# Group norm statistics spread over four slots, with the input loaded earlier, in a pre-activation lookup-convolution block

## The chip, the cores and the metric

The kernel runs on one core of one Trainium2 chip. The core has five engines that each work through their own queue of instructions in order: TensorE (PE), which multiplies matrices into PSUM; VectorE (DVE); ScalarE (ACT); GpSimd (POOL); and SyncE (SP), which here only starts transfers. POOL starts transfers too. The engines wait for one another through semaphores. The metric is the time of one execution on the device in microseconds (us).

## What is computed

For 16 images of 256 channels and 28 x 28 pixels the block takes a group norm of x, passes it through two 3x3 "lookup" convolutions, scales by a squeeze-and-excitation gate and adds x twice:

```python
def amm_conv3x3(x, centroids, w_sub, stride=1):      # C=256, k=16, s=9
    patches = jax.lax.conv_general_dilated_patches(x, (3, 3), (stride, stride), 'SAME')
    p = patches.reshape(B, C, s, Ho * Wo).transpose(0, 3, 1, 2)
    d = (jnp.sum(p * p, axis=-1)[..., None] - 2.0 * jnp.einsum('bncs,cks->bnck', p, centroids)
         + jnp.sum(centroids * centroids, axis=-1)[None, None])
    attn = jax.nn.softmax(-d, axis=-1)
    lut = jnp.einsum('cks,cso->cko', centroids, w_sub)
    out = jnp.einsum('bnck,cko->bno', attn, lut)
    # ...
def _gn(v, G=32, eps=1e-5):
    g = v.reshape(B_, G, C_ // G, H_, W_)
    m = jnp.mean(g, axis=(2, 3, 4), keepdims=True)
    s = jnp.var(g, axis=(2, 3, 4), keepdims=True)
    return ((g - m) / jnp.sqrt(s + eps)).reshape(v.shape)
# block(v):  out = relu(bn1(amm_conv3x3(v)));  out = bn2(amm_conv3x3(out));  out = se(out);  relu(out + v)
# result:    x + block(_gn(x))
```

A group is 8 channels of 784 pixels. With 128 channels on the partitions, its statistics need a reduction along each partition (DVE) and one across 8 partitions (PE, a product with a block-diagonal matrix).

## The kernel before

The kernel is written as a plan of jobs. Each job has a slot and a position within the slot; when the plan is laid out, the jobs are emitted in the order of slot and position, and each lands at the end of its own engine's queue. A stage (one convolution of one image) has 16 slots, one per unit of 32 channels and half the pixels. Stages of layer 0 and layer 1 alternate, so an image takes 32 slots.

```python
LOGITS, LOAD, MOVE, EXP, LOOK_A, NUM, TURN, SMALL, LOOK_B, MAX, LOOK_C, TURN_BACK, REST = range(13)
NS = len(PXT) * NQ                                    # 16
...
# for a unit at slot s:
at(s, LOGITS, b_logits, u)          # PE, L578: 16 matmuls into two PSUM pairs
at(s, EXP, b_exp, u)                # ACT, L636
at(s + 1, NUM, b_num, u)            # PE, L646: 16 matmuls into two PSUM pairs
at(s + 1, TURN, b_turn, u)          # DVE: two transposes out of PSUM (L658), reciprocal (L664)
at(s + 1, TURN, c_scale, u)         # POOL: L674, L680, running sums L686
at(s + 2, TURN_BACK, c_turn, u)     # DVE: L692, for every fourth unit also qt L699
# the products with the tables (PE, L710) of other units lie at LOOK_A, LOOK_B, LOOK_C
```

There are three PSUM pairs in a ring. Logits of one slot and numerators of the next take two each, so a pair must be emptied by ACT or DVE before PE can write it again. The tile of patches (pt) of a unit is loaded by SP three slots ahead; "maxed" units (two per half in layer 1) also go out to DRAM and back (dm) for their maxima.

Group norm of an image runs while the stages of earlier images fill PE. Its parts:

```python
xpool = ctx.enter_context(tc.tile_pool(name="xpool", bufs=2))

def load_x(b, xb):
    t = xpool.tile([P, NB, HW], F32, tag="xt", name="xt")
    nc.gpsimd.dma_start(t, xb.rearrange("(b p) n -> p b n", p=P))      # L148, 784 KB
    xs[b] = t

def gn_stats(b, k):                                                   # DVE
    if k == 0:
        gst[b] = small.tile([P, NB, 2], F32, name="gn_mv")
    st = small.tile([P, 2, 6], F32, name="gn_st")
    for i in range(2):
        nc.vector.bn_stats(st[:, i, :], xs[b][:, k, i * (HW // 2) : (i + 1) * (HW // 2)])   # L428
    nc.vector.bn_aggr(gst[b][:, k, :], st)                            # L429

def gn_mean(b):
    mv = gst[b]
    ps = spare()[:, : 2 * NB]
    nc.tensor.matmul(ps, lhsT=gmat, rhs=mv.rearrange("p b t -> p (b t)"), start=True, stop=True)  # PE, L434
    gm = small.tile([P, NB, 2], F32, name="gn_gm", bufs=6)
    nc.scalar.copy(gm.rearrange("p b t -> p (b t)"), ps)              # ACT, L436
    dv = small.tile([P, NB], F32, name="gn_dv")
    nc.gpsimd.tensor_sub(dv, mv[:, :, 0], gm[:, :, 0])                # POOL, L438
    nc.gpsimd.tensor_mul(dv, dv, dv)                                  # POOL, L439
    gst[b] = gm, dv

def gn_var(b):
    gm, dv = gst.pop(b)
    ps = spare()[:, :NB]
    nc.tensor.matmul(ps, lhsT=gmat, rhs=dv, start=True, stop=True)    # PE, L445
    # ... copy by ACT (L447); add, rsqrt, scale and shift by POOL (L448 to L453)

def gn_apply(b, k):                                                   # ACT, L458
    # ... ims[0] = x * rstd + nb

# in the plan, for image b, t = the anchor:
def norm(self, b, t):
    self.at(t, REST, gn_stats, b, 0)
    self.at(t + 1, REST, gn_stats, b, 1)
    self.at(t + 2, SMALL, gn_mean, b)
    self.at(t + 3, SMALL, gn_var, b)
    self.at(t + 4, REST, gn_apply, b, 0)
    self.at(t + 5, REST, gn_apply, b, 1)

# in the loop over stages, t = 16 * (stage number):
n0 = 3 if b == 1 else t - 2 * NS - 3
plan.at(n0 - (4 if b == 1 else 2), REST, load_x, b, x[b])
plan.norm(b, n0)
```

Image 0 is normalized ahead of the plan, image 1 in its first slots. x of an image is loaded a second time, for the residual, when its layer 1 is done.

Of the kernel before, what the change touches and what calls it, by code (L numbers as in the profile page):

```python
# [8 lines left out]
F32 = mybir.dt.float32  # L9
# [6 lines left out]
P = 128  # L16
H = W = 28
HW = H * W
# [52 lines left out]
def kernel(  # L71
# [32 lines left out]
    nc = tc.nc  # L104
    B, C, _ = x.shape
    NB = C // P
# [5 lines left out]
    small = ctx.enter_context(tc.tile_pool(name="small", bufs=3))  # L112
# [18 lines left out]
    def spare():  # L131

        return ring[(turn[0] + 1) % 3][:, 1]
# [10 lines left out]
    xs = {}  # L144

    def load_x(b, xb):
        t = xpool.tile([P, NB, HW], F32, tag="xt", name="xt")
        nc.gpsimd.dma_start(t, xb.rearrange("(b p) n -> p b n", p=P))  # L148
        xs[b] = t
# [270 lines left out]
    gst = {}  # L420
    nrm = {}

    def gn_stats(b, k):
        if k == 0:
            gst[b] = small.tile([P, NB, 2], F32, name="gn_mv")
        st = small.tile([P, 2, 6], F32, name="gn_st")
        for i in range(2):
            nc.vector.bn_stats(st[:, i, :], xs[b][:, k, i * (HW // 2) : (i + 1) * (HW // 2)])  # L428
        nc.vector.bn_aggr(gst[b][:, k, :], st)  # L429

    def gn_mean(b):
        mv = gst[b]
        ps = spare()[:, : 2 * NB]
        nc.tensor.matmul(ps, lhsT=gmat, rhs=mv.rearrange("p b t -> p (b t)"), start=True, stop=True)  # L434
        gm = small.tile([P, NB, 2], F32, name="gn_gm", bufs=6)
        nc.scalar.copy(gm.rearrange("p b t -> p (b t)"), ps)  # L436
        dv = small.tile([P, NB], F32, name="gn_dv")
        nc.gpsimd.tensor_sub(dv, mv[:, :, 0], gm[:, :, 0])  # L438
        nc.gpsimd.tensor_mul(dv, dv, dv)  # L439
        gst[b] = gm, dv  # L440
# [300 lines left out]
    LOGITS, LOAD, MOVE, EXP, LOOK_A, NUM, TURN, SMALL, LOOK_B, MAX, LOOK_C, TURN_BACK, REST = range(13)  # L741

    class Plan:
# [82 lines left out]
                self.at(t + 6 if dx == 1 else t + 7 + 3 * h + (i - n * h - NB) * 3 // 4, REST, to_pat, l, i, pat, *PXT[1])  # L826

        def norm(self, b, t):
            self.at(t, REST, gn_stats, b, 0)
            self.at(t + 1, REST, gn_stats, b, 1)  # L830
            self.at(t + 2, SMALL, gn_mean, b)
            self.at(t + 3, SMALL, gn_var, b)
            self.at(t + 4, REST, gn_apply, b, 0)
            self.at(t + 5, REST, gn_apply, b, 1)

        def close(self, b, ob, te, pace):
            self.at(te, SMALL, se_hidden, b)
# [12 lines left out]
    NS = len(PXT) * NQ  # L850
# [6 lines left out]
    def pat_of(l, b):  # L857
        return d_pat[2 * l + b % 2]
# [2 lines left out]
    row = sort_keys()  # L861
    square_codes(0)
    for k in range(NB):
        gn_stats(0, k)
    gn_mean(0)
    gn_var(0)
    sort_ranks(row)
# [9 lines left out]
    plan = Plan(1, 3, 6)  # L877
    for si, (l, b) in enumerate(stages):
        t = si * NS
        plan.stage(l, b, pat_of(l, b), t, () if l == 0 else MAXED)  # L880
        if l == 0 and b >= 1:
            n0 = 3 if b == 1 else t - 2 * NS - 3
            plan.at(n0 - (4 if b == 1 else 2), REST, load_x, b, x[b])
            plan.norm(b, n0)
            plan.prep(0, pat_of(0, b), {1: 9, 2: 33, 3: 57}.get(b, t - 2 * NS + 3), 0.67 if b == 1 else 1)
        if l == 1:
            if b in (0, B - 1):
                plan.prep_near(1, pat_of(1, b), t - NS + LC)
            else:
                plan.prep(1, pat_of(1, b), 45 if b == 1 else t - 2 * NS + LC + 1)  # L890
            plan.at(t + NS, REST, load_x, b, x[b])
            plan.close(b, out[b], t + NS + LC, 1 if b < B - 2 else 4)
# [25 lines left out]
    for i, lim in enumerate((S_MAX, 1.0 / S_MIN)):  # L918
        t = small.tile([P, 1], F32, name="ext")
# [9 lines left out]
    with tc.If(flag > 0):  # L929
        with tc.For_i(0, B) as bi:  # L930
            load_x("g", x[bass.ds(bi, 1)].rearrange("o c n -> (o c) n"))
            plan = Plan(8, 3, 6)
            plan.norm("g", 0)
            plan.prep(0, d_pat[0], 8)
            s0 = 32
            plan.stage(0, "g", d_pat[0], s0, range(NQ))
            plan.prep(1, d_pat[2], s0 + plan.end)
            s1 = s0 + plan.end + 24
            plan.stage(1, "g", d_pat[2], s1, range(NQ))
            plan.at(s1 + plan.end - 4, REST, load_x, "g", x[bass.ds(bi, 1)].rearrange("o c n -> (o c) n"))  # L940
            plan.close("g", out[bass.ds(bi, 1)].rearrange("o c n -> (o c) n"), s1 + plan.end, 1)
            plan.emit()
# [74 lines left out]
```

## Time and profile before

| | |
|---|---|
| time, median of three | 2895.39 us (2892.28 to 2902.37) |
| profiled span | 2894.4 us |
| PE busy | 2797.8 us, 97% |
| DVE busy | 2258.5 us, 78% |
| POOL busy | 1766.8 us, 61% |
| ACT busy | 1090.3 us, 38% |
| statistics passes (L428) | 64, mean 545 ns |
| aggregations (L429) | 32, mean 209 ns |
| load of x, issue to landing | 8.9 us in the median, 10.8 at most |

The profile names an instruction by its line, engine, operation and tiles, out<-in. Busy time is the union of an engine's instructions; idle time before an instruction is put down to whatever released it. A row of the waits reads "engine tile line <- what ended the wait: total us, times, longest us". A busy PE is not one at its peak, since matmuls overlap and their ends are modelled. The clock row gives the share of TensorE's full clock that was granted.

### The profile page before, as it was taken

What the parts mean: (1) busy time and instruction counts of PE and PEld (TensorE: products, weight loads), DVE (VectorE), ACT (ScalarE), POOL (GpSimd) and SP (SyncE); (2) the same over time, 40 slices, a digit from 0 to 9 for tenths busy, and PEclk for the clock granted to TensorE, in tenths of its full rate; (3) what the DMA queues carried; (4) which work ended last, traced back from release to release, by engine and by line L of the source; (5) the groups of instructions that cost most, each with busy time, mean ns of one, the idle gap of its engine ahead of it and who ended that gap; (6) DMA issues with size and microseconds to landing.
All of it is one profiled execution on the core that took longest, in us unless ns stands there. A gap on an engine that the chain in (4) does not pass through costs nothing.

```text
span 2894.4 us, 94782 instructions
## 1 busy us (share of the span) xinstructions
PE 2797.8 (97%) x39834; PEld 1105.5 (38%) x39834; DVE 2258.5 (78%) x2770; ACT 1090.3 (38%) x1595; POOL 1766.8 (61%) x2577
## 2 busy tenths in 40 slices
PE   6998999999999999999999999999999999999996
PEld 3433333333333333333333333333333333333332
DVE  4575888787877878788787877878788787878885
ACT  2332343433434343343433434343343434333332
POOL 3564675666756566675656656566665656656653
PEclk9999999999999999999999999999999999999998
DMA  8776878867767676776767767686776767774651
GB/s 230 193 181 173 208 219 207 221 159 212 192 173 200 153 220 173 198 200 154 217 161 202 190 177 191 158 224 163 216 191 163 204 156 215 185 186 119 154 134 57
DMA packets 296643, 530.27 MB, mean 183 GB/s; under 512 B 94240, under 2 KB 251632, under 8 KB 296208
## 3 DMA queue, kind: packets, MB, share of 16 engines
q0 software_dynamic: 51616, 269.48, 34.8%
q1 hardware_dynamic: 244592, 254.65, 34.5%
q8 instruction: 315, 5.16, 0.8%
q14 instruction: 120, 0.98, 0.1%
HBM read 269.96 MB, written 254.05 MB: 181 GB/s over the span
## 4 chain that ended last, share of the span: by engine, by line
PE 77%; DMA 9%; POOL 6%; issue 4%; DVE 3%; ACT 0%; SPq 0%; POOLq 0%; DVEq 0%; ACTq 0%
PE acc L710 49%; PE pair L578 15%; PE pair L646 13%; DMA xt<-in_x 4%; DMA pt<-pat 3%; POOL k L674 2%; POOL total L686 1%; DVE nt L658 1%; POOL pat L479 1%; POOL tail L680 1%; DVE rc L664 1%; DVE gn_st L428 1%; DMA pat<-side 1%; PE pair L335 1%; DMA part<-in_wsub 0%
## 5 line engine op out<-in xcount | busy, mean ns | idle before, releaser
L710 PE MATMUL acc<-q,ws 128*128 128x384 f32 (+1 forms) x4096 | 1648.1, 520 | 2.3 <-ACT y L732 2.3
L674 POOL TENSOR_TENSOR k<-nt,rc 128x832 f32<-128x832 f32 (+1 forms) x512 | 802.5, 1567 | 1079.0 <-DVE rc L664 1058.9
L658 DVE STREAM_TRANSPOSE nt<-pair 128x832 f32<-128x832 f32 (+1 forms) x1024 | 978.9, 994 | 524.6 <-PE pair L646 405.2
L636 ACT ACTIVATE e<-pair 128x800 f32<-128x800 f32 (+1 forms) x1024 | 789.5, 821 | 1414.7 <-PE pair L578 1368.9
L710 PEld LDWEIGHTS acc<-q,ws 128*128 128x128 f32 x4096 | 699.0, 190 | 900.3 <-issue 578.9
L578 PE MATMUL pair<-pt,wd 19*32 19x384 f32 (+2 forms) x18432 | 575.6, 501 | 33.7 <-DVE nt L658 18.1
L692 DVE STREAM_TRANSPOSE q<-k 128x832 f32<-128x832 f32 (+1 forms) x512 | 488.9, 955 | 0.8 <-POOL k L674 0.8
L646 PE MATMUL pair<-e,cw 32*32 32x384 f32 (+1 forms) x16384 | 485.1, 501 | 0.3 <-DVE nt L658 0.2
L664 DVE RECIPROCAL rc<-nt 128x104 f32<-128x104 f32 (+1 forms) x512 | 398.7, 779 | 17.6
L578 PEld LDWEIGHTS pair<-pt,wd 19*32 19x32 f32 (+1 forms) x18432 | 141.7, 103 | 379.0 <-issue 279.4
L680 POOL TENSOR_TENSOR tail<-nt,rc 128x104 f32<-128x104 f32 (+1 forms) x512 | 236.7, 462 | 0.0
L646 PEld LDWEIGHTS pair<-e,cw 32*32 32x32 f32 x16384 | 119.9, 103 | 290.2 <-issue 146.5
L710 PE MATMUL acc<-qt,ws 128*128 128x400 f32 (+1 forms) x512 | 221.9, 515 | 0.0
L686 POOL TENSOR_TENSOR total<-total,nt 128x96 f32<-128x96 f32 (+1 forms) x448 | 197.3, 440 | 0.0
L479 POOL DMA_DIRECT2D pat<-side x274 | 184.4, 673 | 3.4 <-ACT side L468 3.0
L686 POOL TENSOR_TENSOR total<-total,rc 128x96 f32<-128x96 f32 (+1 forms) x448 | 176.3, 394 | 0.0
L710 PEld LDWEIGHTS acc<-qt,ws 128*128 128x128 f32 x512 | 91.9, 192 | 101.1 <-issue 52.8
L602 DVE TENSOR_REDUCE mx<-z 128x48 f32<-128x768 f32 (+1 forms) x128 | 120.6, 942 | 0.0
L597 DVE STREAM_TRANSPOSE z<-pair 128x768 f32<-128x768 f32 (+1 forms) x128 | 118.1, 961 | 0.1
L479 POOL DMA_DIRECT2D pat<-im x136 | 91.8, 675 | 0.0
L732 ACT ACTIVATE y<-acc,bnsh,bnsc 128x384 f32<-128x384 f32 (+1 forms) x64 | 43.4, 678 | 86.9 <-PE acc L710 81.8
L544 POOL TENSOR_TENSOR y<-y,xt 128x392 f32<-128x392 f32 x60 | 65.9, 1099 | 10.4 <-ACT y L540 10.4
(109 smaller groups left out, 738.8 us busy)
## 6 DMA issues: line engine op xcount, KB each, us to landing
pat<-side POOLq DMA_DIRECT2D x232, 588.0 KB, 5.9
pt<-pat SPq DMA_DIRECT2D x1024, 112.5 KB
pt<-pat SPq DMA_DIRECT2D x1024, 108.0 KB
pat<-im POOLq DMA_DIRECT2D x116, 588.0 KB, 6.0
xt<-in_x POOLq DMA_DIRECT2D x32, 784.0 KB, 8.9
out_dram<-y POOLq DMA_DIRECT2D x16, 784.0 KB, 6.3
pat<-side POOLq DMA_DIRECT2D x24, 300.0 KB, 6.2
pat<-side POOLq DMA_DIRECT2D x18, 288.0 KB, 5.5
```

What stands on the lines that cost most here:

```text
L479: eng.dma_start(view(pat, (ROWS * p0 + 9 * k + 3 * dx) * HW + px, [[ROWS * HW, m], [HW, 3], [1, n]]), bass.AP(v.tensor, v.offset, [list(v. ...
L578: nc.tensor.matmul(ps[t // 2][c : c + 32, t % 2, :n], lhsT=wd[l][32 * i : 32 * i + rows, 4 * u["m"] + t, :], rhs=u["pt"][32 * i : 32 * i + ...
L602: nc.vector.tensor_reduce(u["mx"][:, 2 * v : 2 * v + 2].rearrange("p t (j b) -> p t b j", j=2)[:, :, :nb], u["z"].pop(0)[:, : 64 * nb].rea ...
L636: nc.scalar.activation(e[:, :, :n], ps[:, :, :n], AF.Exp, scale=2.0)
L646: nc.tensor.matmul(u["nm"][t // 2][32 * i : 32 * i + 32, t % 2, :n], lhsT=cw[l][c : c + 32, 4 * u["m"] + t, :], rhs=es[t // 2][c : c + 32, ...
L658: nc.vector.transpose(nt[:, :nb, 2 * v : 2 * v + 2].rearrange("p b t r -> p t b r"), ps[:, :, : 32 * nb].rearrange("p t (b r) -> p t b r", ...
L664: nc.vector.reciprocal(rc[:, : 8 * nb], u["nt"][:, :, SUM])
L674: nc.gpsimd.tensor_tensor(q[:, :nb].rearrange("p b (a s) -> p (b a) s", s=8), nt[:, :, :8], rc.unsqueeze(2).to_broadcast([P, 8 * nb, 8]), ...
L680: nc.gpsimd.tensor_tensor(tails[key][:, :nb, 8 * (m % 4) : 8 * (m % 4) + 8], nt[:, :, 8].rearrange("p (b a) -> p b a", a=8), rc.rearrange( ...
L686: nc.gpsimd.tensor_add(t[:, : 8 * nb], t[:, : 8 * nb], v)
L692: nc.vector.transpose(q[:, :, : 32 * nb].rearrange("p h (b r) -> p h b r", r=32), u.pop("k")[:, :nb].rearrange("p b (h r) -> p h b r", h=2),)
L710: nc.tensor.matmul(accs[key][:, :n], lhsT=ws[l][:, 2 * m + h if h < 2 else 2 * NQ + m // 4, o * P : (o + 1) * P], rhs=u["q"][h][:, :n], st ...
```

## The change

The statistics of an image are cut into four jobs of one pass each, in four successive slots, in place of two jobs of two passes. The product of the variances comes two slots after that of the means, where it came one slot after. x is loaded eleven slots ahead of the anchor in place of two; the anchor itself moves four slots later and now stands for the normalization. The aim is to give each step of the chain x, statistics, means, variances more room, and to take less time from DVE in any one slot. The operations themselves, their number and sizes are those of before; the passes of both channel blocks now write into one tile.

```diff
-    def gn_stats(b, k):
-        if k == 0:
-            gst[b] = small.tile([P, NB, 2], F32, name="gn_mv")
-        st = small.tile([P, 2, 6], F32, name="gn_st")
-        for i in range(2):
-            nc.vector.bn_stats(st[:, i, :], xs[b][:, k, i * (HW // 2) : (i + 1) * (HW // 2)])
-        nc.vector.bn_aggr(gst[b][:, k, :], st)
+    def gn_stats(b, k, i):
+        if (k, i) == (0, 0):
+            gst[b] = small.tile([P, NB, 2], F32, name="gn_mv"), small.tile([P, NB, 2, 6], F32, name="gn_st")
+        mv, st = gst[b]
+        nc.vector.bn_stats(st[:, k, i, :], xs[b][:, k, i * (HW // 2) : (i + 1) * (HW // 2)])
+        if i == 1:
+            nc.vector.bn_aggr(mv[:, k, :], st[:, k])
 
     def gn_mean(b):
-        mv = gst[b]
+        mv, _ = gst[b]
...
         def norm(self, b, t):
-            self.at(t, REST, gn_stats, b, 0)
-            self.at(t + 1, REST, gn_stats, b, 1)
-            self.at(t + 2, SMALL, gn_mean, b)
-            self.at(t + 3, SMALL, gn_var, b)
-            self.at(t + 4, REST, gn_apply, b, 0)
-            self.at(t + 5, REST, gn_apply, b, 1)
+
+            for n, (k, i) in enumerate((k, i) for k in range(NB) for i in range(2)):
+                self.at(t - 7 + n, REST, gn_stats, b, k, i)
+            self.at(t - 3, SMALL, gn_mean, b)
+            self.at(t - 1, SMALL, gn_var, b)
+            for k in range(NB):
+                self.at(t + k, REST, gn_apply, b, k)
...
-            n0 = 3 if b == 1 else t - 2 * NS - 3
-            plan.at(n0 - (4 if b == 1 else 2), REST, load_x, b, x[b])
+            n0 = 7 if b == 1 else t - 2 * NS + 1
+            plan.at(n0 - (8 if b == 1 else 11), REST, load_x, b, x[b])
             plan.norm(b, n0)
```

The remaining lines of the diff adapt the two other callers (image 0, and a fallback loop that does not run on these inputs) to the new signature and anchor.

More of the change, by code (lines that the diff above doesn't have):

```diff
@@ L863 @@
     for k in range(NB):
-        gn_stats(0, k)
+        for i in range(2):
+            gn_stats(0, k, i)
     gn_mean(0)
@@ L932 @@
             plan = Plan(8, 3, 6)
-            plan.norm("g", 0)
+            plan.norm("g", 4)
             plan.prep(0, d_pat[0], 8)
```

## The prediction

> **What bounds the kernel now.** I read the page's first part, then the list of waits for TensorE (PE) alone, then the busy time slot by slot over one image, then the chain that ended last and the timelines of PE and VectorE (DVE) in the two slots that stood out.
>
> The page's first part and its clock row:
>
> ```profile
> PE 2797.8 (97%) x39834; PEld 1105.5 (38%) x39834; DVE 2258.5 (78%) x2770; ACT 1090.3 (38%) x1595; POOL 1766.8 (61%) x2577
> PEclk9999999999999999999999999999999999999998
> ```
>
> PE is busy for 2797.8 of 2894.4 us. All that any rearrangement can win, short of making the matmuls cheaper, lies in the 96.6 us of idle PE, plus what PE loses at a lower clock. The waits of PE say who owns the idle time (columns: total us, times, longest us):
>
> ```profile
> PE pair L578 <- DVE nt L658: 18.1, 15, 2.0
> PE pair L445 <- POOL gn_dv L439: 17.4, 14, 1.3
> PE pair L578 <- DMA pt<-pat: 9.3, 6, 3.8
> PE pair L271 <- DVE scratch L270: 9.1, 1, 9.1
> PE pair L335 <- DMA part<-in_wsub: 8.5, 1, 8.5
> PE pair L923 <- DVE good L921: 7.5, 1, 7.5
> ```
>
> The first two rows recur once per image; the rest are the start (before 270 us) and the very end. In windows of one slot (5.4 us) over the image that spans 675 to 858 us, 32 of 34 slots have PE busy throughout, and two do not (columns after the window: length, then busy us and count of PE, PEld, DVE, ACT, POOL, clock, DMA share, GB/s):
>
> ```profile
> 685.80:691.20 5.40, 5.40 (x82) 1.91 (x88) 3.52 (x6) 1.57 (x2) 2.67 (x3) 1.00 0.90 306
> 691.20:696.50 5.30, 4.08 (x54) 1.56 (x70) 5.23 (x9) 1.68 (x2) 1.47 (x1) 1.00 0.79 258
> 696.50:701.90 5.40, 5.40 (x106) 2.05 (x75) 4.16 (x6) 1.67 (x3) 3.60 (x7) 1.00 0.84 261
> 701.90:707.30 5.40, 4.13 (x64) 1.83 (x43) 3.69 (x4) 1.11 (x3) 4.18 (x8) 1.00 0.81 226
> ```
>
> The chain through these two slots names both causes (start us, length us, what):
>
> ```profile
> 680.80 10.15 DMA xt<-in_x
> 690.97 1.05 DVE gn_st L428 x2
> 692.18 1.00 DVE nt L658
> 693.23 0.91 PE pair L578 x16
> ...
> 703.30 0.20 POOL gn_dv L439
> 703.55 0.38 PE pair L445 x2
> ```
>
> First hole, 1.22 us: x is issued two slots before its statistics and lands 10.15 us later. DVE had finished its other work of that slot at 689.12, stood still for 1.85 us (to 690.97), did two passes and an aggregation (1.25 us), and only then emptied the PSUM pair which PE's next logits need. Second hole, 1.27 us: the product of the variances (L445) is next in PE's order at about 702.3, but POOL, which runs nearly two slots behind PE, squares the difference of the means only at 703.50.
>
> [...] PE's timeline after the image at 1556 us (start, length, what)
>
> ```profile
> 1556.39 0.91 PE L578 MATMUL pair<-pt,wd 19*32 19x400 f32 x16 [1.94 <-DVE nt L658]
> 1557.23 1.70 PE L710 MATMUL acc<-q,ws 128*128 128x400 f32 x2
> 1558.72 1.54 PE L710 MATMUL acc<-qt,ws 128*128 128x400 f32 x2
> ```
>
> Two L710 matmuls take 1.70 and 1.54 us there, against 0.94 and 0.83 after the same stall at 693 us. [...] x took 10.15 us to land in a stretch with a DMA share of 0.96, against 8.9 us in the median.
>
> **The change, part by part.** The work is the same: per image four passes (545 ns each), two aggregations (209 ns), two pairs of small matmuls, one load of x. Nothing is added; only places move. Counted in the image's own slots, where 13 is the first slot of statistics before: the load goes from 11 to 6 (nine slots relative to the anchor, five on the clock, since the anchor moves by four); the statistics from 13 and 14 to 10, 11, 12, 13; the means' product from 15 to 14; the variances' product stays in 16; the normalization stays in 17 and 18.
>
> 1. *The x wait.* Issue moves to about 680.8 - 5 x 5.4 = 653.8 us, landing near 664. DVE comes to the first pass in slot 10, near 689.1 - 3 x 5.4 = 673. About 9 us of slack, so the stall on L658 goes. Of its 18.1 us, 1.5 us (two waits, after 2800 us) belong to the end of the last image: 13 waits, **16.6 us**.
>
> 2. *The variance wait.* L445 now comes two slots after L434. POOL has the square a slot (5.4 us) sooner, against 1.27 us missing: the stall goes. Of its 17.4 us, 0.8 us is the first image's, before the pipeline; the other 13 of about 1.28 us make **16.6 us**. (In the second normalization of the pipeline another matmul hides it.)
>
> 3. *The half clock.* Following the long stalls by PE's timeline, four of the 13 are followed by slow matmuls: the six L710 matmuls take 3.81 us (at 148 us), 3.90 (1557), 3.90 (1731) and 3.35 (2249), against 2.21 us at 694; at 2252 the L646 group takes another 0.45 us. The sum over is 1.60 + 1.69 + 1.69 + 1.59 = **6.6 us**, which goes with the stalls.
>
> 4. *A new wait, on L434.* The fourth pass is now in slot 13 and the means' product in slot 14. In the trace, the L658 of slot 13 starts at 684.91, and its slot ends with the qt transpose at 689.12. A pass and an aggregation after it take 0.75 us, so the means are ready at about 689.85. PE is at that place, after its L646 group of slot 14, at 689.57. So PE waits about 0.3 us for gn_mv, where it did not wait before (697.00 against 697.16 us, a margin of 0.16). 14 x 0.3 = **4 us given back**.
>
> 5. *The passes in slots 10 to 12.* DVE's idle time before L658 in the next slots is 1.67, 1.22 and 1.80 us. Against it stand 0.55, 0.75 and 0.55 us. They fit, the tightest by 0.5 us. No cost.
>
> Sum: 16.6 + 16.6 + 6.6 - 4 = 35.8 us. From the median of 2895.4 this leaves **2860 us** (-1.2%).
>
> **The rivals.** *A: the wait moves to the means.* If semaphores or DVE jitter make step 4 cost 1 us per image in place of 0.3, 14 us are given back and the time is near 2870. For it: the margin is already negative by my count. Against it: slot 12 leaves DVE 1.2 us of slack, so it enters slot 13 on time. *B: the earlier x load delays others.* At 654 us it could hold up the loads of patches and of the maxima, pt<-pat and pt<-dm, that maxed tiles wait for; 1 us per image gives 2875. Against it: SyncE's own queue shows a hole just there,
>
> ```profile
> 646.26 5.33 SPq L565 DMA_DIRECT2D pt<-pat  x8
> 664.32 1.55 SPq L617 DMA_DIRECT2D dm<-mt  x2
> ```
>
> with nothing issued between 651.6 and 664.3, while the load before fell into the burst that follows. If anything this relieves. It speaks for B that images 2 and 3 are loaded amid set-up traffic, where PE already waits for pt (9.3 us): a few us either way. *C: DVE becomes the bound.* With 139.9 us busy of 172.6 (the image from 681.0 to 853.6 us) it isn't on average, and step 5 shows the slots; I give it little. *D: only one stall goes,* because the second is fed by another chain (the copy by ACT, POOL's running sums in front of the square): then about 2877. *E: more than the sum,* if POOL and DVE, no longer delayed, also shorten waits at the start: 2850.
>
> **Range and chances.** The sum without step 4 is 2856, with rival A or B 2870 to 2875, with D 2877; the runs before spread from 2892 to 2902, some 4 us around the median. Range 2848 to 2877. To pass 2% the kernel would have to reach 2837.5 us, 58 us less, more than the two stalls and the clock together hold (39.8 us): 3%. Slower by over 2% would need a new stall of 7 us per image: 1%.
>
> **What would show it.** Right: the waits list of PE has no L445 <- POOL gn_dv row and next to nothing of L578 <- DVE nt ; DVE gn_st <- DMA xt (25.5 us before) is gone; PE's busy time stays near 2795; a small row L434 <- DVE gn_mv of 3 to 6 us appears; no half-clock matmuls in mid-kernel; the period per image falls from 172.6 to about 170. Wrong: an L434 row over 10 us (A), new pt rows after 270 us (B), L445 still there (D), or a period that falls without the rows changing.

## The result

The changed kernel takes 2852.3 us in the median of three runs (2847.2 to 2856.5) against 2895.4 before: a ratio of 0.985, 95% interval 0.981 to 0.988. On the chip of a later experiment it was 2847.4 against 2899.6, 0.983 (0.981 to 0.985). So it is faster, by less than 2%; 43 us in the first comparison, where 36 were predicted. The time lies near the lower end of the range of 2848 to 2877 us, that of the second comparison just below it.

The page after, first part:

```profile
PE 2777.7 (98%) x39834; PEld 1099.2 (39%) x39834; DVE 2256.4 (79%) x2770; ACT 1087.4 (38%) x1595; POOL 1767.5 (62%) x2577
```

PE's idle time fell from 96.6 to 68.0 us (2845.7 - 2777.7), as predicted. But its *busy* time fell too, by 20 us, with the same 39834 instructions; 6.6 us of that was foreseen, as the end of the half clock (the four stretches that the prediction counts, at 148, 1557, 1731 and 2250 us, are 3.413 us long each, at a granted clock of 0.50). The waits of PE, between 300 and 2700 us, where image after image is alike (total us, times, longest us), in the kernel before:

```profile
PE pair L445 <- POOL gn_dv L439: 16.6, 13, 1.3
PE pair L578 <- DVE nt L658: 14.6, 12, 2.0
PE pair L578 <- DMA pt<-dm: 0.4, 1, 0.4
PE pair L578 <- issue: 0.3, 1, 0.3
```

and after:

```profile
PE pair L434 <- DVE gn_mv L429: 4.5, 13, 0.6
PE pair L578 <- DMA pt<-dm: 0.2, 1, 0.2
```

Both old rows are gone, and the new one on the means is there. The wait gn_st <- DMA xt, 25.5 us before, has no row any more. The chain through the place where the holes were now stays on PE but for one passage through DVE (start us, length us, what):

```profile
678.46 0.90 DVE q L692
679.37 0.49 DVE qt L699
679.85 0.46 DVE gn_st L427
680.32 0.02 issue
680.34 0.22 DVE gn_mv L429
680.56 0.14 issue
680.69 0.36 PE pair L434 x2
```

**Where the further busy time went.** PE's timeline at the first hole before (start, length, what, idle time ahead of it):

```profile
691.11 0.90 PE L578 MATMUL pair<-pt,wd 19*32 19x400 f32 x16
693.23 0.91 PE L578 MATMUL pair<-pt,wd 19*32 19x400 f32 x16 [1.22 <-DVE nt L658]
694.06 0.94 PE L710 MATMUL acc<-q,ws 128*128 128x400 f32 x2
```

and at the same group after:

```profile
682.43 0.95 PE L578 MATMUL pair<-pt,wd 19*32 19x400 f32 x32
683.31 0.94 PE L710 MATMUL acc<-q,ws 128*128 128x400 f32 x2
```

Whole, the group holds PE for 683.31 - 682.43 = 0.88 us until the next group starts. Split by the wait it held PE for 694.06 - 691.11 = 2.95 us. The stall therefore cost 2.07 us, not the 1.22 us that its row shows. (The profile has 32 records for the 16 matmuls of a group; 16 records fill one PSUM pair.) The first 16 records are drawn 0.90 us long, but the last of them starts at 691.52, and the next one only at 693.23: what is drawn after 691.52 is the modelled tail of a pipeline that gets nothing new, and it counts as busy. Below, the **cost** of a stall always means this: the time from the start of a group to the start of the next, less the median of that time over groups of the same kind and size in the same trace; costs of over 0.15 us are counted.

Summed over 300 to 2700 us, the costs before are 25.7 us for 13 waits in L578 groups (of 14.6 us of rows, and 0.3 put down to issue), 17.5 us for 13 waits ahead of L445 (16.6), and 5.0 us of half clock. After, they are 5.4 us for 13 waits ahead of L434 (4.5), and none at half clock. So they fall by 42.8 us. This can be checked without rows or medians: the L578 group that starts at 299.5 us before starts 3.05 us sooner after, and the one at 2699.05 us starts 47.36 us sooner, so that 44.3 us were won in between.

### The profile page after: what moved, and what is told of

The parts are those of the page before. It is cut to its first block, busy times and chain, and to the rows that moved or that the text cites. A ratio compares the mean times of both kernels' runs of the same rounds, so it can differ in the third digit from the quotient of the medians.

```text
span 2845.7 us, 94797 instructions
## 1 busy us (share of the span) xinstructions
PE 2777.7 (98%) x39834; PEld 1099.2 (39%) x39834; DVE 2256.4 (79%) x2770; ACT 1087.4 (38%) x1595; POOL 1767.5 (62%) x2577
## 4 chain that ended last, share of the span: by engine, by line
PE 90%; DMA 4%; DVE 3%; issue 1%; POOL 1%; SPq 0%; ACT 0%; DVEq 0%; POOLq 0%; ACTq 0%
PE acc L710 57%; PE pair L578 17%; PE pair L646 15%; DMA pt<-pat 2%; DVE nt L658 1%; DMA part<-in_wsub 1%; DVE q L692 1%; DVE rc L664 1%; DMA pt<-dm 0%; PE pair L335 0%; DMA pat<-side 0%; PE pair L507 0%; DVE gn_st L427 0%; DVE qt L699 0%; DMA dws<-part 0%
## 5 line engine op out<-in xcount | busy, mean ns | idle before, releaser
L658 DVE STREAM_TRANSPOSE nt<-pair 128x832 f32<-128x832 f32 (+1 forms) x1024 | 979.2, 994 | 499.8 <-PE pair L646 444.4
L636 ACT ACTIVATE e<-pair 128x800 f32<-128x800 f32 (+1 forms) x1024 | 787.8, 821 | 1393.0 <-PE pair L578 1339.5
L578 PE MATMUL pair<-pt,wd 19*32 19x384 f32 (+2 forms) x18432 | 564.1, 501 | 15.6 <-DMA pt<-pat 7.8
L646 PE MATMUL pair<-e,cw 32*32 32x384 f32 (+1 forms) x16384 | 485.2, 501 | 0.3 <-DVE nt L658 0.2
L578 PEld LDWEIGHTS pair<-pt,wd 19*32 19x32 f32 (+1 forms) x18432 | 139.9, 103 | 350.6 <-issue 277.0
L646 PEld LDWEIGHTS pair<-e,cw 32*32 32x32 f32 x16384 | 119.8, 103 | 288.8 <-issue 158.0
L732 ACT ACTIVATE y<-acc,bnsh,bnsc 128x384 f32<-128x384 f32 (+1 forms) x64 | 43.4, 678 | 86.8 <-PE acc L710 81.8
```

The source lines that it names most:

```text
L578: nc.tensor.matmul(ps[t // 2][c : c + 32, t % 2, :n], lhsT=wd[l][32 * i : 32 * i + rows, 4 * u["m"] + t, :], rhs=u["pt"][32 * i : 32 * i + ...
L636: nc.scalar.activation(e[:, :, :n], ps[:, :, :n], AF.Exp, scale=2.0)
L646: nc.tensor.matmul(u["nm"][t // 2][32 * i : 32 * i + 32, t % 2, :n], lhsT=cw[l][c : c + 32, 4 * u["m"] + t, :], rhs=es[t // 2][c : c + 32, ...
L658: nc.vector.transpose(nt[:, :nb, 2 * v : 2 * v + 2].rearrange("p b t r -> p t b r"), ps[:, :, : 32 * nb].rearrange("p t (b r) -> p t b r", ...
```

## The experiments

Times are medians beside runs of the kernel before on the same chip; a ratio is to that kernel, with its 95% interval.

### Only the earlier load

```diff
-            plan.at(n0 - (4 if b == 1 else 2), REST, load_x, b, x[b])
+            plan.at(n0 - (4 if b == 1 else 7), REST, load_x, b, x[b])
```

> Kernel before with one edit: x of images 2 to 15 is loaded five slots sooner; statistics, means and variances stay where they were. Theory (the first stall is the late load, and it costs more than its idle row shows, because the first half of the split L578 group counts as busy while it drains: about 2.1 us each, 27.7 us for 13, plus 6.6 us of half clock): the gn_st <- DMA xt wait and the L578 <- DVE nt rows in mid-kernel go, L445 <- POOL gn_dv stays at 13 x 1.28 us, perhaps 0.2 us per image on L434; about 31 us off, near 2864. Rival 1 (the cost is what the idle rows show): 16.6 + 6.6 - 3 = 20 us off, near 2875. Rival 2 (two passes in one slot stall PE even with x at hand): an L578 <- DVE nt row of about 1 us per image stays, near 2880.

2862.4 against 2898.6 us, 0.988 (0.986 to 0.990). 36 us off: nearest to the theory (31), not rival 1 (20 us) or rival 2. PE's waits from 300 to 2700 us:

```profile
PE pair L445 <- POOL gn_dv L439: 16.5, 13, 1.3
PE pair L578 <- DMA pt<-dm: 0.5, 2, 0.3
```

The variances still wait, and the L578 row is gone with two passes per slot. DVE's timeline shows why two passes are no burden once x is there:

```profile
683.47 0.99 DVE L428 BATCH_NORM_STATS2 gn_st<-xt 128x6 f32<-128x392 f32 x2
684.50 0.21 DVE L429 BATCH_NORM_AGGREGATE gn_mv<-gn_st 128x2 f32<-128x12 f32 x1
684.62 1.94 DVE L658 STREAM_TRANSPOSE nt<-pair 128x832 f32<-128x832 f32 x2
```

Without the 1.85 us of standing still, L658 frees the pair about when PE asks for it: PE's L578 group there starts at 685.53 and the next at 686.52, a cost of 0.11 us. The costs between 300 and 2700 us fall from about 50 to 18.3 us. Image 2, which lies earlier, has its own stall before: its row showed 2.02 us, its cost is about 2.9 with the tail, and 1.6 us of half clock follow. Together this makes 36 us, the difference of the medians. That they agree so closely is partly luck: the two profiles are 33.6 us apart, and only 1.6 us of this lie ahead of 300 us, where the set-up also changes from run to run.

### Only the lag of two slots

```diff
-            self.at(t + 3, SMALL, gn_var, b)
-            self.at(t + 4, REST, gn_apply, b, 0)
-            self.at(t + 5, REST, gn_apply, b, 1)
+            self.at(t + 4, SMALL, gn_var, b)
+            self.at(t + 5, REST, gn_apply, b, 0)
+            self.at(t + 6, REST, gn_apply, b, 1)
```

> Kernel before with one edit: the variances' product two slots behind the means' in place of one, the normalization one slot later with it; x loaded as before, two passes per slot as before. Theory: L445 <- POOL gn_dv goes (13 x 1.35 us = 17.5 us), the L578 <- DVE nt rows stay at 13 of about 1.3 us; near 2878. Rival (the square is late because POOL itself is late, and the lateness returns elsewhere): L445 moves, but the wait turns up at another instruction of PE, and the time stays near 2895.

2889.0 against 2898.6 us, 0.997 (0.996 to 0.998): 10 us, between the theory (17.5) and the rival (none). L445's row is gone:

```profile
PE pair L578 <- DVE nt L658: 13.5, 12, 2.0
PE pair L578 <- DMA pt<-dm: 0.7, 1, 0.7
PE pair L578 <- issue: 0.6, 1, 0.6
```

but 0.89 us came back in 12 of the 13 images (0.17 in one) at a place without a row, 10.9 us in all. ACT's timeline there:

```profile
543.97 0.68 ACT L732 ACTIVATE y<-acc,bnsh,bnsc 128x400 f32<-128x400 f32 x1 [1.58 <-PE acc L710]
...
544.64 1.03 ACT L458 ACTIVATE im<-xt,gn_nb,gn_rstd 128x784 f32<-128x784 f32 x1
545.58 0.81 ACT L468 COPY side<-im 128x756 f32<-128x756 f32 x1
546.29 1.50 ACT L636 ACTIVATE e<-pair 128x768 f32<-128x768 f32 x2
```

and PE's:

```profile
543.86 0.93 PE L578 MATMUL pair<-pt,wd 19*32 19x384 f32 x32
544.72 1.56 PE L710 MATMUL acc<-q,ws 128*128 128x384 f32 x4
546.20 1.82 PE L646 MATMUL pair<-e,cw 32*32 32x384 f32 x32
547.95 0.35 PE L494 MATMUL pair<-ysum,w_sb 128*16 128x1 f32 x8
```

In this edit the second normalization (L458) falls into the slot in which the preparation of patches begins (L468). Both stand ahead of the exponentials (L636) in ACT's queue, and ahead of both stands L732, which had waited 1.58 us for PE. The exponentials start 1.5 us after their logits are done, and PE's L646 group takes 1.75 us to the next start in place of 0.86. The second half of that group writes a pair which those exponentials must read first: it starts at 547.14, just after the first of the two ends (547.09). So the rival is half right for this edit: much of the wait turns up at another instruction of PE, but through ACT and the delayed normalization, not through a late POOL. The change leaves the normalization where it was. In the next experiment L458 and L468 also follow one another directly, without L732 in front of them, and no loss of this size is seen: the meeting of these two alone does not make it.

### The split and the lag, with the load as late as before

```diff
-            n0 = 7 if b == 1 else t - 2 * NS + 1
-            plan.at(n0 - (8 if b == 1 else 11), REST, load_x, b, x[b])
+            n0 = 7 if b == 1 else t - 2 * NS + 4
+            plan.at(n0 - (8 if b == 1 else 9), REST, load_x, b, x[b])
...
-            plan.prep(0, pat_of(0, b), {1: 9, 2: 33, 3: 57}.get(b, t - 2 * NS + 3), 0.67 if b == 1 else 1)
+            plan.prep(0, pat_of(0, b), {1: 9, 2: 33, 3: 57}.get(b, t - 2 * NS + 5), 0.67 if b == 1 else 1)
```

> Changed kernel with the load put back: x of images 2 to 15 is issued two slots before its first pass, as before, and the whole chain of passes, means, variances, normalization and preparation stands two to three slots later. Four passes in four slots and the lag of two remain. Theory: DVE still waits about 1.85 us for x, then one pass (0.55 us) in place of two and an aggregation (1.25 us), so the first stall shrinks by 0.7 us from 2.1 to about 1.4 us per image; L445 gone; 17.5 + 9 us off plus some of the half clock, near 2866. Rival (the split alone is worth the gain): near 2852, the time of the whole change. Rival (the load alone is): near 2878.

2866.5 against 2898.6 us, 0.990 (0.987 to 0.992), as the theory had it. DVE still waits 26.9 us for x in all. The L578 <- DVE nt row shows 6.3 us between 300 and 2700 us; the cost is 17.1 us for 13 stalls, 1.3 us each. With x as late as before, smaller pieces thus save 25.7 - 17.1 = 8.6 us.

### Passes one slot sooner

```diff
-                self.at(t - 7 + n, REST, gn_stats, b, k, i)
+                self.at(t - 8 + n, REST, gn_stats, b, k, i)
...
-            n0 = 7 if b == 1 else t - 2 * NS + 1
-            plan.at(n0 - (8 if b == 1 else 11), REST, load_x, b, x[b])
+            n0 = 8 if b == 1 else t - 2 * NS + 1
+            plan.at(n0 - (9 if b == 1 else 12), REST, load_x, b, x[b])
```

> Changed kernel with the four passes and the load one more slot sooner, so that the means' product comes two slots after the last pass. Theory: the L434 <- DVE gn_mv row between 300 and 2700 us goes, 14 x 0.38 us = 5 us off the changed kernel, near 2847. Rival (the waiting PE comes back one group later, because VectorE is equally late for its next transpose): the same time as the changed kernel.

2843.2 us, 0.982 (0.980 to 0.984), where the changed kernel on the same chip took

> The changed kernel again, on the chip that the next kernels run on: near 2852, with L434 <- DVE gn_mv at 0.32 us in each image and no other wait of PE between 300 and 2700 us.

2847.4 us, 0.983 (0.981 to 0.985). Beside the L434 row, its trace has two small waits that were not expected, 0.9 us for ACT's y and 0.4 us for pt <- dm. The intervals overlap, so the times alone do not show a gain. In the traces the L434 row is gone: with the passes sooner, this one row is all that PE waits for between 300 and 2700 us,

```profile
PE pair L578 <- DMA pt<-dm: 0.3, 1, 0.3
```

and the costs there fall from 7.0 us (changed kernel, same chip; 5.4 of them ahead of L434) to 0.5. The medians differ by 4 us, about the size of that row.

### What a stall costs, measured by making one

```diff
             plan.norm(b, n0)
+            if b >= 2:
+                plan.at(n0 - 2, REST, delay, b, 8)
...
+    def delay(b, n):
+        st = small.tile([P, 8, 6], F32, name="dl_st")
+        for i in range(n):
+            nc.vector.bn_stats(st[:, i, :], xs[b][:, 0, : HW // 2])
```

> Changed kernel with eight more passes (8 x 0.55 = 4.4 us of VectorE, their result unused) in one slot of images 2 to 15, the slot before the variances' product; it measures what a stall of PE in the middle of an L578 group costs against what the waits show. Theory (the waits show too little, since the half group in front drains as busy): an L578 <- DVE nt row of about 1.2 us per image, and about 2.0 us per image in time, 28 us over the changed kernel, near 2880. Rival (the row is the cost): time over the changed kernel equals the sum of the rows, about 16 us, near 2868.

2888.6 us, 41 us over the changed kernel on the same chip; the rows of PE between 300 and 2700 us (lines are five higher here: L583 is L578, L663 is L658, L439 is L434):

```profile
PE pair L583 <- DVE nt L663: 15.3, 13, 1.2
PE pair L439 <- DVE gn_mv L429: 4.2, 13, 0.3
PE pair L583 <- DMA pt<-dm: 1.2, 2, 1.1
```

PE's timeline at one of them:

```profile
706.24 0.87 PE L583 MATMUL pair<-pt,wd 19*32 19x384 f32 x16
708.29 0.88 PE L583 MATMUL pair<-pt,wd 19*32 19x384 f32 x16 [1.18 <-DVE nt L663]
709.10 2.28 PE L715 MATMUL acc<-q,ws 128*128 128x400 f32 x6
...
714.57 1.61 PE L715 MATMUL acc<-q,ws 128*128 128x400 f32 x4
716.11 1.36 PE L651 MATMUL pair<-e,cw 32*32 32x384 f32 x32
717.40 1.61 PE L715 MATMUL acc<-q,ws 128*128 128x400 f32 x4
```

The row says 1.18 us; the cost is 709.10 - 706.24 - 0.86 = 2.00 us, the same in all 13. Six of the 13 stalls are followed by 3.4 us at half clock, at 1.69 us each. After the other seven, as here, a further 0.43 us is lost two slots on, in an L651 group (L646 before) that never shows a gap: 1.29 us to the next start in place of 0.86. Here too its second half starts (716.59) just after the first of ACT's two exponentials ends (716.54), and the normalization (714.80 to 715.84) stood ahead of them, in all seven cases. Between 300 and 2700 us the terms are 13 x 2.00 + 6 x 1.69 + 7 x 0.43 = 39 us, against 16 by the rows; from the L578 group at 300.2 us to the one at 2699.4 us of the changed kernel, PE takes 38.9 us longer here. (Image 2 lies ahead of 300 us.) The theory's 28 us lacked the second and the third term; the rival is out.

### Without the split

```diff
-                self.at(t - 7 + n, REST, gn_stats, b, k, i)
+                self.at(t - 6 + k, REST, gn_stats, b, k, i)
```

> Changed kernel without the split: both passes of a channel block in one slot, as before, in the two slots 11 and 12, so that the means' product again comes two slots after the last pass; load and lag of the changed kernel. Theory (early load and lag are worth everything, the split nothing; the split's last pass even causes the L434 wait): no wait of PE of over 0.2 us between 300 and 2700 us, the time of the kernel with earlier passes, near 2843. Rival (two passes in one slot push VectorE over the slot): an L578 <- DVE nt row of 0.3 us or more per image, with about twice that in time, 2850 to 2860.

> The kernel with passes and load one slot sooner, again, on the same chip as the kernel without the split: near 2843, no wait of PE of over 0.4 us between 300 and 2700 us.

2844.1 us (0.982, 0.979 to 0.985) without the split, 2843.8 us (0.982, 0.979 to 0.985) with passes sooner. The time of the second is as expected, its waits are not: in this trace PE waits 2.1 us for pt <- dm (1.8 at most), 1.2 us for an issue and 0.8 us for ACT's y, which the earlier trace of the same kernel doesn't have. Such rows come and go from one execution to the next; none belongs to the group norm, and L434 has none in either. Between 300 and 2700 us PE's rows without the split are

```profile
PE pair L578 <- DMA pt<-dm: 0.9, 3, 0.4
PE pair L578 <- issue: 0.2, 1, 0.2
```

The four slots bring nothing that two don't, as long as the last pass stands two slots ahead of the means' product.

## Why the prediction was right, and where it was short

The two stalls went for the reasons given. What failed is the premise under the sizes: that all there is to win lies in PE's idle time and in the half clock. The busy time was to stay near 2795 us and came to 2777.7; 43 to 52 us were gained, more than the 39.8 us that the stalls and the clock were said to hold.

**Step 1, the x wait: mechanism right, size too small.** The load alone removes it. The step took the term from the waits list, 16.6 us; the costs are 25.7 us for images 3 to 15 and about 2.9 for image 2, some 28.6 us. This is the mis-sized term of the sum, 12 us short. The profile page itself says that the ends of matmuls are modelled; the split group, drawn as 0.90 and 0.91 us in place of 0.95 for the whole, showed it.

**Step 2, the variance wait: right.** 16.6 us of rows, 17.5 of cost. Here the whole group in front had its second half issued, so only 0.07 us per stall was hidden. The row left, and nothing came back, because the normalization kept its slots; the experiment that moved it lost 10.9 of 17.5 us to ACT. No run has this lag alone with the normalization in its old place.

**Step 3, the half clock: right.** No half-clock stretch is left between 270 and 2790 us, where the granted clock is 1.00; 6.6 us were set, and in the experiment with the delay each stretch cost the same 1.69 us.

**Step 4, the new wait on L434: right,** 0.32 us in twelve of the 13 images between 300 and 2700 us and 0.61 in one; 5.4 us in all by cost. The experiment with earlier passes takes it away; the 4 us between the medians lie within their intervals.

**Step 5, slots 10 to 12: right.** No wait there; moreover the split is not needed once x is early.

With all steps at their cost the sum is 28.6 + 17.5 + 6.6 - 5.8 = 47 us (5.8 with the 0.4 us of image 2), against 43 and 52 us in the two comparisons of medians and 48.7 us between the two profiles.

**The rivals.** A fell: 0.32, not 1 us. B fell: x takes less time to land (8.6 us in the median, 10.1 before, for images 2 to 15), and pt <- dm shows 0.2 us. (The 8.9 us that the prediction sets beside 10.15 is the median of all 32 loads before, half of which are the second loads for the residual. Among the loads that the change moves the one of 10.15 us was an ordinary one, so these figures do not show what a DMA share of 0.96 does to a load.) C and D fell. E, more than the sum, came true in part of its size but not for its reason: ahead of 300 us only 3.0 us were won, less than image 2's own stall and half clock; mid-kernel stalls were dearer than their rows.

## What to carry to other kernels

On a saturated engine, size a stall by the distance from the start of one group to the start of the next against the same distance where nothing waits, not by the idle time in a waits list; a wait in the middle of a pipelined group hid 0.8 us here, and some stalls (0.43 and 0.89 us) had no row at all. Where an in-order queue waits for a small side chain, look first at how early its input is issued and how many slots lie between its links; splitting the work into smaller pieces saved 8.6 us while the input was late and nothing once it was there. When such a chain moves, see what its last link pushes aside on its own engine.

## What was not expected of the hardware

Half clock followed stalls of PE that were shorter than it: in the experiment with the delay, stalls of 2.0 us, equal to the hundredth, were followed by 3.4 us of half clock in six of 13 cases. The trace's clock records put the starts of the six at 880.9, 1055.0, 1399.7, 1744.5, 2089.2 and 2434.0 us. The distances from each to the next are multiples of 3.413 us to within 0.1 us (51 and 101 of them), and so are those between the three mid-kernel stretches before (1557.3, 1731.3 and 2250.2 us: 51 and 152). 3.413 us is also the length of each of these three, at a granted clock of 0.50.

The 13 equal stalls also show a pattern. Their L583 groups begin at different places on a grid of 3.413 us laid through the six starts: the six that were followed by half clock 0.11 to 0.49 us after a grid point, the other seven 0.55 to 2.89 us after one, with no exception. So among these equal stalls, the place on the grid went with the half clock. No run set this place on purpose, so whether it decides is not shown.
